# Second cross-attention of a fused network: projection pieces between a step's halves, and two buffers for an unused output

## The chip, the core and the metric

The kernel runs on one core of a Trainium2 chip. A core has TensorE (PE; its weight loads are listed as PEld), VectorE (DVE), ScalarE (ACT), GpSimd (POOL) and SyncE (SP, which here only issues DMAs). Each engine works through its own queue in order; engines wait for each other by semaphores. Products land in PSUM, which has eight banks. The metric is the device time of one execution in microseconds (us). Before the change it is 2459.25 us, the median of 3 runs (2456.62 to 2461.36).

## What is computed

The network has twelve blocks over x (128 tokens of 256). Four of them are cross-attentions over a context of 12,544 keys. The change concerns the second, whose reference, cut to what matters, is:

```python
K = (K_in @ Wk + bk)  # K_in = V_in = context, 12544 x 256; 16 heads of 16
V = (V_in @ Wv + bv)
Q = (Q_in @ Wq + bq)  # Q_in = layernorm(x), 128 x 256
KQ = einsum('bhld,bhpd->bhlp', K, Q) / sqrt(16)
KQ = KQ + mask_pad.reshape(b, 1, l, 1) + mask_attn.T.reshape(1, 1, l, lp)
alpha = softmax(KQ, axis=2)              # over the 12544 keys
O = einsum('bhlp,bhld->bhpd', alpha, V)
return O.transpose(0, 2, 1, 3).reshape(b, lp, 256) @ Wo + bo
```

`mask_attn` is a matrix of 128 x 12544 that is added to the scores of every head. The other three cross-attentions have no such matrix, and so need no addition to each score tile.

## The kernel before

Everything is fp32 and stays on one core. `cross` (from L355) runs one cross-attention. It takes four heads at a time, called a unit, and the keys in tiles of 512: 4 units of 25 tiles, or 100 tiles. The softmax needs each row's maximum before it can exponentiate, so each tile is scored twice:

- `score_s` (L470) computes scores with queries on the partitions, only to find the maximum over the tile for each head. In the second attention (`side`) VectorE adds the mask tile `f` and takes the maximum in one custom instruction (L491); its elementwise result goes to a tile named `junk`, which nobody reads. The profile shows L491 as CUSTOM_DVE_ANT_0 followed by DVE_READ_ACCUMULATOR2_ANT, which writes the maximum.
- `score_t` (L518) computes the same scores with keys on the partitions, 27 tiles later (`lead = NST + 2`, L364), when the unit's maxima are known and have been put into the queries by `lower` (L510). VectorE adds the transposed mask tile `g` (L541), and ScalarE exponentiates (L546).
- `values` (L572) multiplies the exponentials of the tile before with the value tiles (L588), and VectorE adds the result to a sum (L592, L594).

Each tile is one step of the loop at L618. In a step that does both kinds of scoring, `scores` (L549) works in two halves. The first scores heads 2 and 3 for the maxima and heads 0 and 1 for the exponentials; the second does the reverse. A half issues all its products and then all its drains: two L491 and two L541 on VectorE, two L546 on ScalarE. Steps 0 to 26 do maxima alone, steps 27 to 99 both, steps 100 to 126 exponentials alone. A head has 16 rows plus some for mask and maximum in a strip of 32, so four heads fill PE's 128 rows, and products of different heads can run side by side.

The keys and values themselves must be projected from the context. That work is cut into pieces, listed for all four attentions in `self.jobs`, and `pump` (L142) issues as many pieces as it is told. A key piece (`keys`, L201) projects 128 features for 512 keys: four matmuls with all 128 rows of PE (L315), an eviction on ScalarE (L209), and after every second piece a store to DRAM from GpSimd (L212). A value piece (`values`, L214) projects 256 keys: eight matmuls, an eviction (ScalarE in the second attention, L232), and a store after two pieces (L237). The second attention first pumps what is left of its own pieces and then pieces of the third, at a rate written out in L1316.

The order is written by hand: inside `tc.manual_schedule()` (L615) the instructions stand on each engine in the order in which the code issues them. In a step before the change this is: fetches for two tiles ahead, both halves of `scores`, `lower` at the end of a unit, the pieces, `values`.

PSUM banks are dealt out in rotation: `bank` (L135) gives the next of eight. A matmul that writes a bank waits until the engine that drains what lay there is done. A step with one piece takes ten banks: four for the first half, four for the second, one for the piece, one for `values`.

```python
sets = [[(score_s, km, (2, 3)), (score_t, ke, (0, 1))],
        [(score_s, km, (0, 1)), (score_t, ke, (2, 3))]]
for part in sets:
    parts = [make(k, heads) for make, k, heads in part]
    for products, _ in parts:
        products()
    for _, drain in parts:
        drain()
```

Of the kernel before, what the change touches and what calls it, by code (L numbers as in the profile page):

```python
# [25 lines left out]
NST = -(-S2 // ST)  # L26
# [51 lines left out]
class Net:  # L78
# [276 lines left out]
    def cross(self, name, side=False, project=True, rate=()):  # L355
# [11 lines left out]
        with ExitStack() as es:  # L367
# [8 lines left out]
            def rows(u):  # L376

                at = 32 * (width * u % 4)
                return slice(at, at + 32 * width)
# [40 lines left out]
            def fetch_k(k):  # L420

                u, i = divmod(k, NST)
                if u >= units:
                    return
                s, m = i * ST, min(ST, S2 - i * ST)
                if s % SB == 0:
                    b = s // SB
                    self.until(name, b, "k")
                    n = min(SB, S2 - b * SB)
                    clear(NSB * u + b + 2)  # L430
                    t = kts[(NSB * u + b) % held]
                    nc.sync.dma_start(
                        out=t[1::32, :n],
                        in_=self.mask_rows[name][:, s : s + n].to_broadcast([4, n]))
                    for j in range(width):
                        at, h = 32 * j + 2, width * u + j
                        nc.sync.dma_start(out=t[at : at + 16, :n],
                                          in_=self.kx[name, b][16 * h : 16 * h + 16, :])
                    kt[u, b] = t
                if side:  # L440
                    f = ep.tile([P, ST], F32, name=f"{name}_f{k}", tag="f", bufs=3)
                    nc.sync.dma_start(out=f[:, :m], in_=self.io["fside"][:, s : s + m])
                    ft[k] = f
# [21 lines left out]
            def tile_of(u, j):  # L465

                at = 32 * ((width * u + j) % 4)
                return slice(at, at + 32)

            def score_s(k, heads):  # L470

                u, i = divmod(k, NST)
                s, m = i * ST, min(ST, S2 - i * ST)
                if u not in mxs:
                    mxs[u] = pool.tile([P, width, NST], F32, name=f"{name}_mxs{u}", tag="mxs",
                                       bufs=2)
                t, at = kt[u, s // SB], s % SB
                banks = {j: self.bank(f"{name}_s{k}_{j}") for j in heads}

                def products():  # L480
                    for j in heads:
                        r = tile_of(u, j)
                        nc.tensor.matmul(banks[j][:, :m], qb[u][r, :], t[r, at : at + m],  # L483
                                         start=True, stop=True)

                def drain():
                    for j in heads:
                        if side:
                            junk = ep.tile([P, ST], F32, name=f"{name}_j{k}_{j}", tag="junk",
                                           bufs=1)  # L490
                            nc.vector.tensor_tensor_reduce(  # L491
                                out=junk[:, :m], in0=banks[j][:, :m], in1=ft[k][:, :m], scale=1.0,
                                scalar=-3.0e38, op0=ALU.add, op1=ALU.max,
                                accum_out=mxs[u][:, j, i : i + 1])
                        else:
                            nc.vector.tensor_reduce(out=mxs[u][:, j, i : i + 1],  # L496
                                                    in_=banks[j][:, :m], axis=AX.X, op=ALU.max)
                return products, drain

            def raised(k):  # L500

                u, i = divmod(k, NST)
                if i == NST - 1:
                    mx = self.small.tile([P, width], F32, name=f"{name}_mx{u}", tag="mx")
                    nc.vector.tensor_reduce(out=mx, in_=mxs[u], axis=AX.X, op=ALU.max)
                    nc.vector.tensor_scalar(
                        out=lows[u % 2][:, rows(u)].rearrange("p (j r) -> p j r", r=32)[:, :, 0],
                        in0=mx, scalar1=-1.0, scalar2=None, op0=ALU.mult)

            def lower(u):  # L510

                r = rows(u)
                ps = self.bank(f"{name}_mr{u}")
                nc.tensor.matmul(ps[:, :P], lows[u % 2], self.ident, start=True, stop=True)
                nc.vector.tensor_tensor(out=qb[u][r, :], in0=qb[u][r, :], in1=ps[r, :P],
                                        op=ALU.add)
# [29 lines left out]
                        nc.scalar.activation(e[:, j, :m], src, AF.Exp)  # L546
                return products, drain

            def scores(ke, km):  # L549

                if ke is None and km is None:
                    return
                heads = tuple(range(width))
                if ke is None:
                    sets = [[(score_s, km, heads)]]
                elif km is None:
                    sets = [[(score_t, ke, heads)]]
                elif width == 2:
                    sets = [[(score_s, km, heads), (score_t, ke, heads)]]
                else:  # L560
                    sets = [[(score_s, km, (2, 3)), (score_t, ke, (0, 1))],
                            [(score_s, km, (0, 1)), (score_t, ke, (2, 3))]]
                for part in sets:
                    parts = [make(k, heads) for make, k, heads in part]
                    for products, _ in parts:
                        products()
                    for _, drain in parts:
                        drain()
                if km is not None:
                    raised(km)  # L570
# [41 lines left out]
            due, total, waiting = 0.0, units * NST, []  # L612
            n_k = 2 * NST
            n_own = n_k + S2 // 256
            with tc.manual_schedule():  # L615
                for k in (0, 1):
                    fetch_k(k)
                for at in range(total + lead + 3):  # L618
                    fetch_k(at + 2)
                    fetch_v(at + 2 - lead)  # L620
                    ke = at - lead if 0 <= at - lead < total else None
                    km = at if at < total else None
                    scores(ke, km)
                    if 0 < at <= total and at % NST == 0:
                        lower(at // NST - 1)


                    left = sum(1 for (n, _, _), _ in self.jobs if n == name)
                    goal = min(n_k, 2 * (at + 6))
                    if at >= lead - 6:  # L630
                        goal = min(n_own, n_k + 2 * (at - lead + 7))
                    self.pump(min(left, max(0, goal - (n_own - left))))
                    phase = max(0, at - 2) // NST
                    due += rate[phase] if phase < len(rate) else 0.0
                    while due >= 1.0:
                        self.pump(1)
                        due -= 1.0


                    while waiting:  # L640
                        u, i = divmod(waiting[0], NST)
                        n = NST - i if NST - i < 2 * batch else batch
                        last = waiting[0] + n - 1
                        if ke is not None and ke - last < behind - batch + 1:
                            break
                        if last > waiting[-1]:
                            break
                        values(waiting[:n])
                        waiting = waiting[n:]
                    if ke is not None:  # L650
                        waiting.append(ke)
                    u, i = divmod(at - lead - 2 - NST, NST)
                    if i == 0 and 0 <= u < units:
                        finish(u)
# [728 lines left out]
def _device_arrays(I):  # L1383
# [15 lines left out]
    def cross(name, q, k, v, o=None):  # L1399
        a[f"w_{name}"] = cat(*(_padded(q.T).T,) if o is None else (_padded(q.T).T, o))  # L1400
        a[f"w_{name}_kv"] = cat(k, v)

    cross("l0x", I["L0_xattn_q_w"].T, I["L0_xattn_k_w"].T, I["L0_xattn_v_w"].T)
    cross("l1x", *(I[f"L1_xattn_W{k}"] for k in "qkvo"))
    cross("l2x", *(I[f"L2_xattn_w{k}"] for k in "qkvo"))
    cross("l3x", *(I[f"L3_xattn_W{k}"] for k in "qkvo"))
    a["w_l0a"] = cat(I["L0_attn_Wq"].T, I["L0_attn_Wk"].T, I["L0_attn_Wv"].T)
# [73 lines left out]
```

## Time and profile before

| what | us |
|---|---|
| median of 3 runs | 2459.25 |
| the profiled execution | 2463.49 |
| its span, first to last instruction | 2461.6 |
| PE busy (modelled ends) | 2324.9 |
| VectorE busy | 1628.7 |
| ScalarE busy | 1150.0 |
| second attention, from its first L491 to its last L541 | 649.5 to 1298.4 |
| of it, steps that do both kinds of scoring | about 752 to 1208 |

The page of a profile gives, for one execution, the busy time of each engine and then groups of instructions: line, engine, operation, what is written and read, the count, the busy time and the mean length of one, and after the bar the time in which the engine sat idle just before them and what ended it. The waits list who waited for whom, in total. The timeline lists instructions in order of time, with start and length. Windows give the busy time of each engine in chosen stretches, with the share of full speed that TensorE's clock was granted and the busy share of the DMA engines. The busy time of PE is no measure of how full it is, since its ends are modelled and overlap; distances between starts are more telling.

### The profile page before, as it was taken

To read this page: it belongs to the slowest core of one execution; us is meant where nothing else is said; L and a number is where in the kernel's file an instruction comes from. 1 tells how busy PE (TensorE), PEld (TensorE's weight loads), DVE (VectorE), ACT (ScalarE), POOL (GpSimd) and SP (SyncE) were. 2 spreads that over 40 slices of the span, in tenths; PEclk is the share of its full clock that TensorE was granted. 3 is DMA by queue.
4 is the path that set the end of the run, shared out by engine and by line. 5 is a ranking of instruction groups with operands and counts; after the bars stand their busy time and mean duration, and the time that the engine had idled before them with its cause. 6 is when DMAs were issued, how large, how long until landed. Compare 5 with 4: busy or idle time off the path is not lost. (4 is left out here: it accounts for less than half of the span.)

```text
span 2461.6 us, 75645 instructions
## 1 busy us (share of the span) xinstructions
PE 2324.9 (94%) x32103; PEld 1716.3 (70%) x32103; DVE 1628.7 (66%) x3503; ACT 1150.0 (47%) x2109; POOL 246.2 (10%) x465
## 2 busy tenths in 40 slices
PE   6999999999899999999998998899999679999969
PEld 3358888876447876666777744478888546888848
DVE  2566688522477788888886734788882769888331
ACT  2213366773214445545582254046668302666832
POOL 2221100001221100000101111200000121000001
PEclk9999999999999999999999998999999888999979
DMA  7766633237779867777765675553322633333216
GB/s 273 263 222 215 208 97 93 69 118 278 259 232 303 275 216 223 229 227 219 223 198 191 211 254 195 165 151 92 92 78 68 231 109 101 91 91 97 63 44 225
DMA packets 191119, 430.29 MB, mean 175 GB/s; under 512 B 26908, under 2 KB 83248, under 8 KB 186688
## 3 DMA queue, kind: packets, MB, share of 16 engines
q1 hardware_dynamic: 154576, 269.26, 36.9%
q0 software_dynamic: 35840, 154.94, 16.8%
q8 instruction: 256, 4.19, 0.7%
q10 hardware_dynamic: 368, 1.25, 0.1%
q14 instruction: 79, 0.65, 0.1%
HBM read 319.18 MB, written 106.16 MB: 173 GB/s over the span
## 5 line engine op out<-in xcount | busy, mean ns | idle before, releaser
L546 ACT ACTIVATE l1x_e<-l1x_e 128x512 f32<-128x512 f32 (+1 forms) x400 | 240.5, 622 | 248.2 <-DVE l1x_e L541 248.2
L491 DVE CUSTOM_DVE_ANT_0 l1x_j<-l1x_s,l1x_f 128x512 f32<-128x512 f32 (+1 forms) x400 | 271.1, 678 | 80.9 <-PE l1x_t L533 29.9
L496 DVE TENSOR_REDUCE l0x_mxs<-l0x_s 128x1 f32<-128x512 f32 (+1 forms) x400 | 244.3, 672 | 97.5 <-PE l0x_s L483 66.0
L546 ACT ACTIVATE l0x_e<-l0x_t 128x512 f32<-128x512 f32 (+1 forms) x400 | 203.2, 594 | 176.9 <-PE l0x_t L533 173.4
L546 ACT ACTIVATE l3x_e<-l3x_t 128x512 f32<-128x512 f32 (+1 forms) x400 | 203.4, 594 | 167.2 <-PE l3x_s L483 92.6
L496 DVE TENSOR_REDUCE l2x_mxs<-l2x_s 128x1 f32<-128x512 f32 (+1 forms) x400 | 243.8, 672 | 36.7 <-PE l2x_t L533 24.3
L546 ACT ACTIVATE l2x_e<-l2x_t 128x512 f32<-128x512 f32 (+1 forms) x400 | 203.4, 594 | 137.2 <-PE l2x_t L533 133.5
L496 DVE TENSOR_REDUCE l3x_mxs<-l3x_s 128x1 f32<-128x512 f32 (+1 forms) x400 | 243.4, 671 | 33.1 <-PE l3x_t L533 23.9
L541 DVE TENSOR_TENSOR l1x_e<-l1x_t,l1x_g 128x512 f32<-128x512 f32 (+1 forms) x400 | 249.9, 671 | 11.3 <-PE l1x_t L533 8.3
L483 PE MATMUL l3x_s<-l3x_kt,l3x_qb 32*128 32x512 f32 (+1 forms) x800 | 202.8, 652 | 7.1 <-DMA l3x_kt<-l3x_kx 3.5
L533 PE MATMUL l1x_t<-l1x_qb,l1x_kt 32*128 32x128 f32 x3136 | 204.3, 284 | 2.7 <-ACT l1x_vs L232 0.6
L483 PE MATMUL l1x_s<-l1x_kt,l1x_qb 32*128 32x512 f32 (+1 forms) x800 | 203.2, 618 | 3.4 <-DMA l1x_kt<-l1x_kx 3.2
L533 PEld LDWEIGHTS l1x_t<-l1x_qb,l1x_kt 32*128 32x128 f32 x3136 | 171.6, 187 | 36.5 <-ACT l2x_ks L209 19.6
L483 PE MATMUL l2x_s<-l2x_kt,l2x_qb 32*128 32x512 f32 (+1 forms) x800 | 189.5, 620 | 5.8 <-DMA l2x_kt<-l2x_kx 5.3
L483 PE MATMUL l0x_s<-l0x_kt,l0x_qb 32*128 32x512 f32 (+1 forms) x800 | 183.5, 614 | 5.6 <-ACT l0x_ks L209 3.8
L533 PE MATMUL l3x_t<-l3x_qb,l3x_kt 32*128 32x128 f32 x3136 | 181.1, 281 | 0.0
L533 PE MATMUL l2x_t<-l2x_qb,l2x_kt 32*128 32x128 f32 x3136 | 180.0, 280 | 0.0
L533 PE MATMUL l0x_t<-l0x_qb,l0x_kt 32*128 32x128 f32 x3136 | 178.9, 279 | 0.0
L533 PEld LDWEIGHTS l3x_t<-l3x_qb,l3x_kt 32*128 32x128 f32 x3136 | 160.8, 187 | 6.5 <-issue 5.0
L533 PEld LDWEIGHTS l2x_t<-l2x_qb,l2x_kt 32*128 32x128 f32 x3136 | 159.8, 186 | 5.9 <-issue 5.0
L533 PEld LDWEIGHTS l0x_t<-l0x_qb,l0x_kt 32*128 32x128 f32 x3136 | 159.1, 186 | 5.9 <-issue 5.0
L588 PEld LDWEIGHTS l1x_p<-l1x_e,l1x_vt 128*32 128x32 f32 x3136 | 82.0, 110 | 51.3 <-DVE l1x_mxs L491 18.9
(599 smaller groups left out, 3665.8 us busy)
## 6 DMA issues: line engine op xcount, KB each, us to landing
l1x_f<-in_fside SPq DMA_DIRECT2D x96, 256.0 KB
l1x_g<-in_fsideT SPq DMA_DIRECT2D x96, 256.0 KB
w<-in_w_l3f POOLq DMA_DIRECT2D x16, 1024.0 KB, 5.1
l0x_vx<-l0x_vs POOLq DMA_DIRECT2D x24, 544.0 KB, 5.5
l0x_vt<-l0x_vx SPq DMA_DIRECT2D x48, 272.0 KB
l1x_vx<-l1x_vs POOLq DMA_DIRECT2D x24, 544.0 KB, 5.9
l1x_vt<-l1x_vx SPq DMA_DIRECT2D x48, 272.0 KB
l2x_vx<-l2x_vs POOLq DMA_DIRECT2D x24, 544.0 KB, 4.8
```

Of the source, the lines that this page charges most:

```text
L483: nc.tensor.matmul(banks[j][:, :m], qb[u][r, :], t[r, at : at + m], start=True, stop=True)
L491: nc.vector.tensor_tensor_reduce(out=junk[:, :m], in0=banks[j][:, :m], in1=ft[k][:, :m], scale=1.0, scalar=-3.0e38, op0=ALU.add, op1=ALU.m ...
L496: nc.vector.tensor_reduce(out=mxs[u][:, j, i : i + 1], in_=banks[j][:, :m], axis=AX.X, op=ALU.max)
L533: nc.tensor.matmul(banks[j][:, a * P : (a + 1) * P], t[r, at + a * P : at + (a + 1) * P], qb[u][r, :], start=True, stop=True)
L541: nc.vector.tensor_tensor(out=e[:, j, :m], in0=src, in1=gt[k][:, : m // P, :].rearrange("p a q -> p (a q)"), op=ALU.add)
L546: nc.scalar.activation(e[:, j, :m], src, AF.Exp)
L588: nc.tensor.matmul(ps[32 * c : 32 * c + 32, :P], lhs, rhs, start=n < 4, stop=n >= len(todo) - 4, skip_group_check=True)
```

## The change

It has two parts, both for the second attention alone.

The tile `junk` gets two buffers in place of one. It is 512 fp32 values for each of 128 partitions, and the memory is there.

The pieces of a step are counted before `scores` is called. In steps that do both kinds of scoring, half of them (rounded up) are issued between the first half and the second, and the others where they were, before `values`. So a single piece moves wholly between the halves, and of two pieces one does. The number of pieces in each step stays. Outside the second attention, and in its steps with one kind of scoring, `inner` is 0.

```diff
                         if side:
                             junk = ep.tile([P, ST], F32, name=f"{name}_j{k}_{j}", tag="junk",
-                                           bufs=1)
+                                           bufs=2)
...
-            def scores(ke, km):
+            def scores(ke, km, between):
...
-                for part in sets:
+                for n, part in enumerate(sets):
+                    if n == 1:
+                        between()
                     parts = [make(k, heads) for make, k, heads in part]
...
-                    scores(ke, km)
-                    if 0 < at <= total and at % NST == 0:
-                        lower(at // NST - 1)
...
-                    self.pump(min(left, max(0, goal - (n_own - left))))
                     phase = max(0, at - 2) // NST
                     due += rate[phase] if phase < len(rate) else 0.0
-                    while due >= 1.0:
-                        self.pump(1)
-                        due -= 1.0
+                    pieces = min(left, max(0, goal - (n_own - left))) + int(due)
+                    due -= int(due)
+                    inner = (pieces + 1) // 2 if side and ke is not None and km is not None else 0
+                    scores(ke, km, lambda: self.pump(inner))
+                    if 0 < at <= total and at % NST == 0:
+                        lower(at // NST - 1)
+                    self.pump(pieces - inner)
```

## The prediction

> **What bounds the kernel now.** The change touches only the second attention, so I read the page's engine rows and groups first, then busy time in windows of that stage, then its timeline, then its waits.
>
> ```profile
> PE 2324.9 (94%) x32103; PEld 1716.3 (70%) x32103; DVE 1628.7 (66%) x3503; ACT 1150.0 (47%) x2109; POOL 246.2 (10%) x465
> ...
> L491 DVE CUSTOM_DVE_ANT_0 l1x_j<-l1x_s,l1x_f 128x512 f32<-128x512 f32 (+1 forms) x400 | 271.1, 678 | 80.9 <-PE l1x_t L533 29.9
> ```
>
> PE at 94% is a share of modelled ends, so it can't settle what binds. L491 has 80.9 us of idle VectorE before it in 400 instructions, of which PE explains 29.9. The windows:
>
> ```profile
> core 0: us, PE busy (x) PEld busy (x) DVE busy (x) ACT busy (x) POOL busy (x), PEclk, DMA share, GB/s
> 650.00:674.00 24.00, 23.54 (x78) 8.61 (x76) 19.92 (x59) 4.54 (x7) 4.49 (x6) 1.00 0.68 221
> 800.00:871.40 71.40, 71.40 (x918) 60.09 (x911) 54.48 (x132) 35.64 (x64) 9.71 (x20) 1.00 0.83 264
> 884.30:921.20 36.90, 36.41 (x480) 26.88 (x479) 34.78 (x95) 16.60 (x30) 0.75 (x1) 0.95 0.66 201
> 966.10:1028.00 61.90, 61.43 (x771) 39.16 (x769) 53.02 (x132) 31.48 (x53) 3.20 (x6) 1.00 0.75 233
> ```
>
> These are four regimes of one stage: maxima alone; two value pieces a step; no piece; on average 1.2 key pieces a step. In the third VectorE is busy 94%, in the fourth 86%. The timeline shows a step of the fourth (start, length, what; in brackets the engine's idle time and what ended it):
>
> ```profile
> 1034.32 0.69 DVE L491 CUSTOM_DVE_ANT_0 l1x_j<-l1x_s,l1x_f 128x512 f32<-128x512 f32 x1 [0.73 <-PE l1x_t L533]
> ...
> 1034.94 0.08 DVE L491 DVE_READ_ACCUMULATOR2_ANT l1x_mxs<- 128x1 f32 x1
> 1035.17 0.69 DVE L491 CUSTOM_DVE_ANT_0 l1x_j<-l1x_s,l1x_f 128x512 f32<-128x512 f32 x1
> ...
> 1035.78 0.08 DVE L491 DVE_READ_ACCUMULATOR2_ANT l1x_mxs<- 128x1 f32 x1
> 1035.78 1.28 DVE L541 TENSOR_TENSOR l1x_e<-l1x_t,l1x_g 128x512 f32<-128x512 f32 x2
> ...
> 1040.29 0.67 ACT L209 ACTIVATE l2x_ks<-l2x_k,cols 128x512 f32<-128x512 f32 x1
> ...
> 1041.01 0.97 PEld L533 LDWEIGHTS l1x_t<-l1x_qb,l1x_kt 32*128 32x128 f32 x16 [0.95 <-ACT l2x_ks L209]
> ```
>
> Two losses stand here. VectorE: after the read of the accumulator the next L491 starts 0.23 us later (1034.94 to 1035.17), but an L541 at once (1035.78). PE: the second half's t products wait until 1041.01 for ScalarE to empty the bank of the previous step's key piece; ScalarE does that only at 1040.29, behind all four exponentials. The waits confirm it as a habit (in total, times, longest):
>
> ```profile
> PEld l1x_t L533 <- ACT l2x_ks L209: 19.6, 30, 0.9
> ```
>
> **Durations** (distances between starts in the timeline). VectorE: an L491 0.616, plus 0.226 more if another L491 follows; an L541 0.60; the sum L594 0.195. A step: 4 x 0.616 + 2 x 0.226 + 4 x 0.60 + 0.195 = 5.51. That is exactly the distance of steps without a piece (895.27 to 900.77). PE: a half alone 1.07 (the maxima regime, 670.49 to 671.56), both halves back to back 1.96 (849.66 to 851.62); a key piece 1.91 (1035.74 to 1037.65); a value piece 1.83 (3.65 for two, 851.62 to 855.27); L588 1.01. ScalarE: an exponential 0.61, a key eviction 0.67.
>
> With these I laid out the order of before by hand: each operation starts when its engine is free, its PSUM bank emptied (eight in rotation) and its input ready. Five key steps with 1, 1, 1, 1, 2 pieces come to 31.0 us; the trace has 5.51, 6.35, 5.51, 6.35, 7.21 = 30.93. Value steps come to 6.66 and 7.28; the trace has 6.63 and 7.35. So the bank account describes this stage, and I use it for the change.
>
> **Second buffer.** No instruction is added. With one buffer, the second L491 of a pair overwrites what the first wrote, and in the program of before it waits for the accumulator read in front of it; with two its wait looks at least one read further back. No L491 without that wait stands in the trace, so the cost is bounded: at most 0.226 saved (it then starts as an L541 does); at least nothing (if the custom instruction must wait for the read anyway); in between 0.15 (the 0.08 of the read stays). I take 0.226, from the nearest row, 1035.78. VectorE's step: 5.51 - 2 x 0.226 = 5.06. The Trainium skill speaks against it: VectorE: DVE Perf Modes, section The DRAIN you can't avoid, says that a semaphore between chained instructions costs nothing extra, since the next one waits for the pipe in any case. By it this part is worth 0; by 1034.94 against 1035.78 it is worth 0.45 a step. The measured row decides; the rule stays as a rival.
>
> **Pieces between the halves.** Number and order of pieces stay: a lone piece goes wholly between the halves, of two pieces one does. VectorE's and GpSimd's orders are unchanged, so its buffer clears and stores of keys and values pass nothing. On SP one load of weights (l3x_kvw, 0.5 MB) moves ahead of five small loads of keys, needed about two steps later: 0. On PE the piece stands before the second half, whose products VectorE waits for; on ScalarE its eviction stands between the first two exponentials and the last two, so behind it wait those two and the next step's L588. The eviction's own input, the piece, ends before the first exponentials do, so it adds only its 0.67.
>
> Laid out for one key piece, from the first half's start: halves 0 and 2.98, piece 1.07, L588 4.05, next step 5.06. VectorE drains the first half from 1.14 to 3.58, waits to 4.12 for the second half, drains it to 6.56, then L594 to 6.76; the next first half was ready at 6.20. VectorE so needs 5.06 too. The piece's eviction now comes 2.4 us earlier than behind four exponentials. Banks: next step's first half takes the piece's bank for a t tile, which costs 0.49 every other step when VectorE runs late. Five steps give 5.62, 5.08, 5.55, 5.08, 6.93 = 28.26, instead of 30.93.
>
> Against this, TensorEngine Tiling (Array Packing), section Key Properties, says that changing the tiling mode drains TensorE; a piece between the halves adds one change from 32 rows to 128 and back. The row's price is 2 x 1.07 - 1.96 = 0.18 a step; by the rule alone no number follows. Taking the halves at half of 1.96 instead gives 27.86.
>
> **Sum over the stage** (step starts read off VectorE's timeline):
> - 46 key steps, 921.3 to 1207.7: 46/5 x (30.93 - 28.26) = 24.6.
> - 17 value steps from 757: mean 6.99, after 2 x 1.07 + 3.66 + 1.01 = 6.81, plus 0.02 of waits: 17 x 0.16 = 2.7.
> - 8 steps without a piece: 8 x 0.45 = 3.6.
> - Maxima alone, 27 steps: the first 8 take 3.36 = 4 x 0.84, PE needs 1.07 + 1.91 = 2.98: 8 x 0.38 = 3.0. After that PE waits for keys (at 674.94 for a load issued at 670.40) and for a context load (714.66); neither hangs on VectorE, so 0 (at most 8 more).
> - The last 27 steps hold no L491 and keep their order: 0.
>
> Sum 33.9. The profiled execution took 2463.5 (span 2461.6 and 1.9 around it): 2429.6. The median of the runs is 4.2 lower: 2425.4, so **2426**. What is late next: PE in the value steps, both engines about equally in the key steps.
>
> **Rivals.**
> 1. The custom instruction is held by the read anyway. Key steps 29.16, so 9.2 x 1.77 = 16.3, and value steps 2.7: 19.0, **2440**. For: the rule above; no unheld L491 in the trace. Against: 1035.78. Chance 0.12.
> 2. Only the buffer pays: the moved piece makes a new wait as long as the old. With the old order and two buffers the layout gives 29.67: 11.6 + 3.6 + 3.0 + 17 x 0.25 = 22.4, **2437**. Chance 0.11.
> 3. More than laid out: halves at 0.98, 27.86 (28.2), value steps 6.63 (6.1), maxima 6, none 3.6: 44, **2415**. Against: the DMA share, 0.83 in the value steps. Chance 0.12.
> 4. Slower: the second half starves VectorE. If the next first half may not run ahead, because the piece's eviction comes too late for its t tile, a step becomes 1.14 + 1.91 + 1.07 + 2.44 + 0.20 = 6.76 against a mean of 6.19: 46 x 0.57 = 26 lost, 7 gained elsewhere, **2478**. It decides where the wait for the eviction grows from a mean of 0.25 to over 0.78 a step. For: ScalarE keeps order, and exponentials wait for VectorE. Against: ScalarE is busy half the time. Chance 0.06.
> 5. No change, because other waits take it all: **2459**, chance 0.03.
>
> **Chances.** The likeliest case has 0.56, its own range 2419 to 2433 (the 0.15 and 0.226 of the buffer, halves between 0.98 and 1.07). Cases 1 to 3 widen it: 2413 to 2443. 0.2% is 4.9 us, about what a measurement can tell from no change. Faster 0.91, same 0.03, slower 0.06.
>
> **What would show it.** Right: the start after an accumulator read is 0 to 0.08 us later for L491 too; steps without a piece 5.06; five key steps about 28.3; the wait of L533's weights for L209 gone or on the first half; L491 waiting about 0.5 us for PE in the middle of a step; value steps all alike near 6.8. Wrong: 0.23 stays (case 1); key steps still alternate with over 6.2 (case 2); L491's wait in mid-step over 1 us (case 4). TensorE's clock was halved for 3.41 us at 1077 (one step took 9.7); if denser work brings more of that, each costs some 2 us.

## The result, and the profile after

The changed kernel took 2430.81 us, the median of 4 runs (2424.94 to 2440.84), against 2458.07 for the kernel before, measured beside it (4 runs, 2456.62 to 2461.36). The ratio is 0.9891, with a 95% interval from 0.9856 to 0.9927. The forecast was 2426, with a range from 2413 to 2443.

The profiled execution took 2424.94, its span 2422.8. That span is 38.8 shorter than the one before, but only 30.9 of it lies in the second attention (649.4 to 618.5, from its first L491 to its last L541). The other 7.9 lie where no instruction was touched, and a second profile of the same kernel, e0_again below, does not have them: there the stretch after the stage takes 1162.5, as before it took 1162.8. So at most the 30.9 are the change's; in e0_again the stage takes 624.6, which is 24.8 less than before.

From the page of the changed kernel (line numbers behind L561 are two higher than before, so L588 is now L590 and L594 is L596):

```profile
PE 2289.4 (94%) x32103; PEld 1699.7 (70%) x32103; DVE 1611.5 (67%) x3503; ACT 1150.0 (47%) x2109; POOL 246.8 (10%) x465
...
L491 DVE CUSTOM_DVE_ANT_0 l1x_j<-l1x_s,l1x_f 128x512 f32<-128x512 f32 (+1 forms) x400 | 253.0, 676 | 74.8 <-PE l1x_t L533 39.7
```

Counts are the same. L491's mean length is too (676 ns against 678), but its group is busy 18.1 us less: the two of a pair now overlap in the record. VectorE waits longer for L533, 39.7 against 29.9: it got faster, and PE is late more often. The windows of the changed kernel, for value steps, steps without a piece, and key steps:

```profile
767.50:866.00 98.50, 98.50 (x1230) 78.84 (x1230) 74.35 (x182) 47.80 (x84) 13.59 (x28) 1.00 0.85 274
879.20:908.40 29.20, 28.84 (x418) 22.43 (x416) 28.61 (x82) 13.90 (x25) 0.00 (x0) 0.94 0.69 213
942.20:1026.80 84.60, 84.60 (x1153) 55.57 (x1152) 77.46 (x197) 47.22 (x79) 4.81 (x9) 1.00 0.83 254
```

VectorE's share rose from 94% to 98% in the steps without a piece, and from 86% to 92% in the key steps. In the value steps it is 75%, after 76%: there it does not bind. The timeline of the changed kernel shows a value step (start, length, what; in brackets idle time and releaser; PE's L533 beside L483 is left out):

```profile
838.13 1.99 PE L315 MATMUL l1x_v<-l1x_kvw,l1x_cv 128*128 128x256 f32 x8
838.19 0.69 DVE L491 CUSTOM_DVE_ANT_0 l1x_j<-l1x_s,l1x_f 128x512 f32<-128x512 f32 x1 [0.73 <-PE l1x_t L533]
...
838.80 0.08 DVE L491 DVE_READ_ACCUMULATOR2_ANT l1x_mxs<- 128x1 f32 x1
838.80 0.69 DVE L491 CUSTOM_DVE_ANT_0 l1x_j<-l1x_s,l1x_f 128x512 f32<-128x512 f32 x1
...
840.06 0.70 PE L483 MATMUL l1x_s<-l1x_kt,l1x_qb 32*128 32x512 f32 x2
...
841.16 1.99 PE L315 MATMUL l1x_v<-l1x_kvw,l1x_cv 128*128 128x256 f32 x8
...
843.08 1.08 PE L590 MATMUL l1x_p<-l1x_e,l1x_vt 128*32 128x128 f32 x32
...
844.09 0.70 PE L483 MATMUL l1x_s<-l1x_kt,l1x_qb 32*128 32x512 f32 x2
```

Two things are to be seen. The second L491 starts with the accumulator read, at 838.80, no longer 0.23 after it. And PE never pauses, yet its starts are further apart than forecast: piece to half 1.93 (838.13 to 840.06), half to piece 1.10, piece to L590 1.92. The same view of PE in a key step:

```profile
979.05 0.70 PE L483 MATMUL l1x_s<-l1x_kt,l1x_qb 32*128 32x512 f32 x2
...
980.15 1.08 PE L590 MATMUL l1x_p<-l1x_e,l1x_vt 128*32 128x128 f32 x32
981.16 0.70 PE L483 MATMUL l1x_s<-l1x_kt,l1x_qb 32*128 32x512 f32 x2
...
982.26 1.98 PE L315 MATMUL l2x_k<-l2x_ck,l2x_kvw 128*128 128x512 f32 x4
984.18 0.70 PE L483 MATMUL l1x_s<-l1x_kt,l1x_qb 32*128 32x512 f32 x2
```

That is 1.10 + 1.01 + 1.10 + 1.92 = 5.13 without a gap: PE sets these steps, with VectorE's 5.03 just behind. The wait of L533's weights for the key eviction fell from 19.6 us in 30 times to 0.6 in two:

```profile
PEld l1x_t L533 <- ACT l2x_ks L209: 0.6, 2, 0.4
```

Stretch by stretch, from the starts on VectorE (us):

| steps | before | after | one step or five, before | after |
|---|---|---|---|---|
| 0 to 26, maxima alone | 102.3 | 99.4 | | |
| 27 to 44, mostly value pieces | 127.0 | 125.0 | 7.35 and 6.63 in turn | 7.07 |
| 45 to 51, no piece | 37.0 | 34.9 | 5.50 | 5.03 |
| 52 to 98, key pieces | 292.0 | 269.0 | five: 30.93 | 28.21 |
| 99 to 126, exponentials alone (99 still both) | 91.1 | 90.3 | | |

The value steps got slower, 7.07 against a mean of 6.99. Their stretch is shorter only because of its first two steps, which took 15.2 before, with TensorE's clock halved at 760, and 12.0 after. Without a halved clock there, e1 and e3 below take 13.0 for them in the old order.

In the maxima steps VectorE now waits for the mask tile `f`. Its waits there (in total, times, longest), before and after:

```profile
DVE l1x_j L491 <- DMA l1x_f<-in_fside: 0.5, 1, 0.5
```

```profile
DVE l1x_j L491 <- DMA l1x_f<-in_fside: 14.3, 7, 3.0
```

One key step, step 93, grew from 7.01 to 10.40. It holds the first value piece of the third attention, and PE stands waiting for that piece's context load:

```profile
1140.63 0.64 PE L533 MATMUL l1x_t<-l1x_qb,l1x_kt 32*128 32x128 f32 x8
1144.07 3.45 PE L315 MATMUL l2x_v<-l2x_kvw,l2x_cv 128*128 128x256 f32 x8 [2.81 <-DMA l2x_cv<-in_ctxT]
```

The load is issued early in the step ahead, as before. Before, PE came to the piece 8.2 us after the issue and found the data there; now it is ready for it after 6.5 us, and the data come after 9.3. The piece then meets a halved clock (3.45 us in place of 1.99). The same wait, of 1.8 to 4.4 us, stands in 11 of the 12 profiles of kernels that move the pieces (e9_four_f has none; in e5_interleaved the profile puts it down to VectorE). It is not in the profile of before, nor in that of e1_buffer_only, which leaves the pieces where they were. So the wait goes with the move, and the forecast has no term for it. Why the data come no sooner, no run shows.

### The profile page after: what moved, and what is told of

It reads as the page before. It is cut to its first block, busy times and chain, and to the rows that moved or that the text cites. A ratio compares the mean times of both kernels' runs of the same rounds, so it can differ in the third digit from the quotient of the medians.

```text
span 2422.8 us, 75640 instructions
## 1 busy us (share of the span) xinstructions
PE 2289.4 (94%) x32103; PEld 1699.7 (70%) x32103; DVE 1611.5 (67%) x3503; ACT 1150.0 (47%) x2109; POOL 246.8 (10%) x465
## 5 line engine op out<-in xcount | busy, mean ns | idle before, releaser
L546 ACT ACTIVATE l1x_e<-l1x_e 128x512 f32<-128x512 f32 (+1 forms) x400 | 240.6, 622 | 219.5 <-DVE l1x_e L541 219.5
L496 DVE TENSOR_REDUCE l0x_mxs<-l0x_s 128x1 f32<-128x512 f32 (+1 forms) x400 | 244.3, 672 | 97.4 <-PE l0x_s L483 66.0
L491 DVE CUSTOM_DVE_ANT_0 l1x_j<-l1x_s,l1x_f 128x512 f32<-128x512 f32 (+1 forms) x400 | 253.0, 676 | 74.8 <-PE l1x_t L533 39.7
L546 ACT ACTIVATE l0x_e<-l0x_t 128x512 f32<-128x512 f32 (+1 forms) x400 | 203.2, 594 | 176.9 <-PE l0x_t L533 173.4
L546 ACT ACTIVATE l3x_e<-l3x_t 128x512 f32<-128x512 f32 (+1 forms) x400 | 203.5, 594 | 166.8 <-PE l3x_s L483 92.3
L546 ACT ACTIVATE l2x_e<-l2x_t 128x512 f32<-128x512 f32 (+1 forms) x400 | 203.3, 594 | 137.3 <-PE l2x_t L533 133.7
L496 DVE TENSOR_REDUCE l2x_mxs<-l2x_s 128x1 f32<-128x512 f32 (+1 forms) x400 | 243.8, 672 | 35.8 <-PE l2x_t L533 23.9
L496 DVE TENSOR_REDUCE l3x_mxs<-l3x_s 128x1 f32<-128x512 f32 (+1 forms) x400 | 243.2, 672 | 33.7 <-PE l3x_t L533 23.9
L541 DVE TENSOR_TENSOR l1x_e<-l1x_t,l1x_g 128x512 f32<-128x512 f32 (+1 forms) x400 | 250.1, 672 | 10.0 <-PE l1x_t L533 9.0
L483 PE MATMUL l3x_s<-l3x_kt,l3x_qb 32*128 32x512 f32 (+1 forms) x800 | 201.4, 653 | 8.3 <-DMA l3x_kt<-l3x_kx 7.8
L483 PE MATMUL l1x_s<-l1x_kt,l1x_qb 32*128 32x512 f32 (+1 forms) x800 | 203.1, 635 | 3.1 <-DMA l1x_kt<-l1x_kx 3.1
L533 PE MATMUL l1x_t<-l1x_qb,l1x_kt 32*128 32x128 f32 x3136 | 202.8, 284 | 0.2
L483 PE MATMUL l2x_s<-l2x_kt,l2x_qb 32*128 32x512 f32 (+1 forms) x800 | 189.6, 617 | 5.5 <-DMA l2x_kt<-l2x_kx 5.0
L483 PE MATMUL l0x_s<-l0x_kt,l0x_qb 32*128 32x512 f32 (+1 forms) x800 | 182.2, 612 | 5.7 <-ACT l0x_ks L209 4.0
L533 PE MATMUL l3x_t<-l3x_qb,l3x_kt 32*128 32x128 f32 x3136 | 181.1, 281 | 0.0
L533 PE MATMUL l2x_t<-l2x_qb,l2x_kt 32*128 32x128 f32 x3136 | 179.9, 280 | 0.0
L533 PE MATMUL l0x_t<-l0x_qb,l0x_kt 32*128 32x128 f32 x3136 | 179.0, 279 | 0.0
L533 PEld LDWEIGHTS l1x_t<-l1x_qb,l1x_kt 32*128 32x128 f32 x3136 | 168.9, 186 | 10.0 <-DVE l1x_e L541 3.2
L533 PEld LDWEIGHTS l3x_t<-l3x_qb,l3x_kt 32*128 32x128 f32 x3136 | 160.8, 187 | 6.5 <-issue 5.0
L533 PEld LDWEIGHTS l2x_t<-l2x_qb,l2x_kt 32*128 32x128 f32 x3136 | 159.8, 186 | 5.9 <-issue 5.0
L533 PEld LDWEIGHTS l0x_t<-l0x_qb,l0x_kt 32*128 32x128 f32 x3136 | 159.2, 186 | 5.9 <-issue 5.0
L590 PE MATMUL l1x_p<-l1x_e,l1x_vt 128*32 128x128 f32 x3136 | 112.5, 278 | 2.0 <-ACT l1x_e L546 1.9
```

Source lines behind the costliest of these rows:

```text
L491: nc.vector.tensor_tensor_reduce(out=junk[:, :m], in0=banks[j][:, :m], in1=ft[k][:, :m], scale=1.0, scalar=-3.0e38, op0=ALU.add, op1=ALU.m ...
L496: nc.vector.tensor_reduce(out=mxs[u][:, j, i : i + 1], in_=banks[j][:, :m], axis=AX.X, op=ALU.max)
L533: nc.tensor.matmul(banks[j][:, a * P : (a + 1) * P], t[r, at + a * P : at + (a + 1) * P], qb[u][r, :], start=True, stop=True)
L541: nc.vector.tensor_tensor(out=e[:, j, :m], in0=src, in1=gt[k][:, : m // P, :].rearrange("p a q -> p (a q)"), op=ALU.add)
L590: nc.tensor.matmul(ps[32 * c : 32 * c + 32, :P], lhs, rhs, start=n < 4, stop=n >= len(todo) - 4, skip_group_check=True)
```

## The experiments

Each kernel computes the whole reference. Diffs are cut, and against the changed kernel unless it is said otherwise. "Five key steps" and "value step" are read from the distances between starts in a stretch that no halved clock touches. Kernels e0 to e3 shared one chip, e4 to e8 another, e8_again to e10 a third, and e11 a fourth.

**e0_again.** No edit: the changed kernel once more, as the measure of what a profile repeats.

> The changed kernel once more, beside the others on one chip. From the trace: key steps 28.2 us for five, value steps 7.07 each, steps without a piece 5.03, the stage 618.5 us from first L491 to last L541 (649.4 before). Theory (two separate losses, each part removes one): 2427 to 2431 us, about 28 to 31 under before. Rival (part of the measured gain is chance in the clock outside the stage): under 25 gained.

2438.92 (2429.82 to 2452.58), before there 2463.75, ratio 0.9904 (0.9875 to 0.9933). Five key steps 28.21, value steps 7.07, no piece 5.03: to 0.01 the same. But the maxima steps took 102.6 (99.4 in the first profile), step 93 took 12.04 (10.40), and the stage 624.6. So steps repeat, and stage lengths differ by some 6 us from one execution to the next. The 28 to 31 expected were missed: 24.8 were gained, 0.2 on the rival's side of its line. The interval, 16.5 to 31, reaches to both sides. Parts below are judged by steps.

**e1_buffer_only.** The order of before, with the second buffer. This diff alone is against the kernel before.

```diff
-                                           bufs=1)
+                                           bufs=2)
```

> Before, with two buffers for the unused output and the old place of the pieces. Theory: VectorE's step falls to 5.03 and the wait of the second half for the eviction stays, so five key steps 29.7 (5.06, 6.3, 5.06, 6.3, 7.0), value steps 6.66 and 6.83, maxima steps as in the changed kernel: about 22 us under before, 2436. Rival (the buffer alone is the change): as fast as the changed kernel, 28 to 31 under before. Rival (the order alone is): no gain.

2441.02 (2439.33 to 2441.86), ratio 0.9905 (0.989 to 0.992). Five key steps 29.54 and 29.73 in turn, 29.63 on average, where the layout gave 29.67; value steps 6.89 and 6.63 in turn; no piece 5.03. The buffer is worth all of its 0.226 per pair. The old loss on PE stays; the waits of this kernel, and its timeline on PE:

```profile
PEld l1x_t L533 <- ACT l2x_ks L209: 14.5, 16, 0.9
```

```profile
991.14 1.04 PE L483 MATMUL l1x_s<-l1x_kt,l1x_qb 32*128 32x512 f32 x4
992.29 1.16 PE L533 MATMUL l1x_t<-l1x_qb,l1x_kt 32*128 32x128 f32 x16
993.38 1.98 PE L315 MATMUL l2x_k<-l2x_ck,l2x_kvw 128*128 128x512 f32 x4
```

The t products of both halves run together, 1.15 after the s products that they could have lain beside. Its time is not told from e0_again's. The steps say why: against the whole change it loses 46/5 x 1.42 = 13 in key steps and gains 17 x 0.31 = 5 in value steps, 8 us net. Some of that returns in step 93: 6.73 here, where PE does not wait for the context load, against 10.40 and 12.04. What is left is within the intervals.

**e2_order_only.** The moved pieces, with one buffer.

```diff
-                                           bufs=2)
+                                           bufs=1)
```

> The changed kernel with one buffer again. Theory: the second half no longer waits for the eviction, but VectorE's 0.226 us after each accumulator read stays, so steps without a piece 5.51, five key steps 29.2, value steps 7.07 (TensorE without a gap, so the buffer counts for nothing there), maxima steps 3.36: about 15 us under before, 2444. Rival (the order alone is the change): 28 under before.

2450.54 (2443.93 to 2462.76), ratio 0.9942 (0.9922 to 0.9962). Five key steps 29.14 (the layout gave 29.16), no piece 5.49, value steps 7.07. So 5.49 to 5.03 is the buffer's, and 7.07 the order's.

**e3_values_after.** Value pieces stay behind both halves; only key pieces move.

```diff
-                    inner = (pieces + 1) // 2 if side and ke is not None and km is not None else 0
+                    inner = (pieces + 1) // 2 if side and ke is not None and km is not None and not left else 0
```

> The changed kernel, but while pieces of the second attention's own values are left, all pieces stay behind both halves. Theory (two value pieces parted by a half cost TensorE 0.44 us a step more than side by side, and that is more than the eviction wait they save): value steps 6.66 and 6.83 in place of 7.07, key steps unchanged at 28.2 for five, so 5 us faster than the changed kernel. Rival (7.07 comes from transfers or from the bank of the piece, not from the place): value steps stay near 7.07, or key steps after them suffer; no gain.

2431.82 (2428.38 to 2437.87), ratio 0.987 (0.9852 to 0.9889). Value steps 6.89 and 6.63, key steps unchanged at 28.21. Moving value pieces costs 0.31 a step.

**e4_both_between.** Both value pieces of a step stand side by side between the halves.

```diff
-                    inner = (pieces + 1) // 2 if side and ke is not None and km is not None else 0
+                    inner = (pieces if left else (pieces + 1) // 2) if side and ke is not None and km is not None else 0
```

> The changed kernel, but both value pieces of a step stand between the halves, side by side. It tells what makes a value step 7.07. Theory (each change between products of 32 and of 128 rows costs TensorE about 0.1 us, so what counts is how often the kinds alternate): two pieces side by side 3.66, two halves of 1.10, L588 1.01: 6.87 to 6.95 a step, key steps unchanged at 28.2, so 2 to 3 us under the changed kernel in the stage. Rival (the bank of the piece or its eviction makes it): 7.07 stays or grows.

2433.33 (2421.49 to 2441.21), ratio 0.9883 (0.9839 to 0.9928). Every value step takes 6.87. Its timeline on PE:

```profile
829.94 0.70 PE L483 MATMUL l1x_s<-l1x_kt,l1x_qb 32*128 32x512 f32 x2
...
831.04 3.72 PE L315 MATMUL l1x_v<-l1x_kvw,l1x_cv 128*128 128x256 f32 x16
834.69 0.70 PE L483 MATMUL l1x_s<-l1x_kt,l1x_qb 32*128 32x512 f32 x2
...
835.79 1.08 PE L590 MATMUL l1x_p<-l1x_e,l1x_vt 128*32 128x128 f32 x32
836.80 0.70 PE L483 MATMUL l1x_s<-l1x_kt,l1x_qb 32*128 32x512 f32 x2
```

Two pieces side by side take 3.65, parted 3.85; the halves still take 1.10 each. PE's packed value step takes 6.63 where halves, pieces and L590 each stand in one run (three changes of kind a step, counting the one into the next step), 6.87 with four changes, 7.07 with five. Each further change costs 0.24 and 0.20.

**e5_interleaved.** One buffer, but each half's drains alternate, so that an L541 stands between two L491.

```diff
-                def drain():
-                    for j in heads:
+                def drain(n=None):
+                    for j in heads if n is None else heads[n : n + 1]:
...
-                                           bufs=2)
+                                           bufs=1)
...
+                    if side and len(parts) == 2:
+                        for j in range(2):
+                            for _, drain in parts:
+                                drain(j)
+                        continue
```

> The changed kernel with one buffer again, but a half's drains alternate: L491, L541, L491, L541. Theory (what costs is only the wait of an L491 for the accumulator read directly in front of it, not the buffer as such): an L541 stands in between, the wait is over when the second L491 comes, steps without a piece 5.03 and five key steps about 28.2, as with two buffers. In the maxima steps there is no L541, so they stay at 3.36. Rival (the custom instruction is slower when it writes the same tile again): 5.49 and 29.1 as with the order alone.

2434.63 (2432.5 to 2440.75), ratio 0.9895 (0.987 to 0.9921). Five key steps 28.21, no piece 5.03: what two buffers give, from one. VectorE's timeline:

```profile
986.82 0.08 DVE L491 DVE_READ_ACCUMULATOR2_ANT l1x_mxs<- 128x1 f32 x1
986.82 0.69 DVE L541 TENSOR_TENSOR l1x_e<-l1x_t,l1x_g 128x512 f32<-128x512 f32 x1
987.42 0.68 DVE L491 CUSTOM_DVE_ANT_0 l1x_j<-l1x_s,l1x_f 128x512 f32<-128x512 f32 x1
```

The loss was the wait on the instruction directly ahead, not the shared memory: with one instruction between, the wait is met before it is reached. In the maxima steps, where nothing can stand between, each step still takes 3.36.

**e7_all_four.** The pieces go between the halves in all four attentions.

```diff
-                    inner = (pieces + 1) // 2 if side and ke is not None and km is not None else 0
+                    inner = (pieces + 1) // 2 if ke is not None and km is not None else 0
```

> The changed kernel with the pieces between the halves in all four cross-attentions. The other three show no wait of the second half for an eviction (their evictions need no addition first). Theory: there the new place only costs what alternating costs, 0.2 to 0.4 us in each step with pieces, about 70 steps each: 30 to 60 us slower than the changed kernel, and slower than before. Rival (the place is good in itself): as fast or faster than the changed kernel.

2447.47 (2438.74 to 2457.29, 11 runs), ratio 0.9942 (0.9925 to 0.9959). The price was right and the count wrong: it was expected to be slower than before, and is faster. In the first attention the value steps go from 6.63 to 7.07 as forecast, but there are only 17 of them, so they cost 17 x 0.44 = 7.5 us and not 30 or more. The stage grows by 10.3 (487.9 to 498.2, from its first L496 to its last L546); 1.8 of that stand in its first step, which no moved piece touches. The third attention grows by 2.5, the fourth by 0.1. In the first attention, where PE sets the value steps, the move only costs.

**e8_evict_first.** PE's order and the banks are those of before (only at the end of a unit do the pieces now stand ahead of `lower`). The pieces are issued behind both halves' products but ahead of the second half's drains, so that only ScalarE's order changes: it empties the piece's bank before the last two exponentials.

```diff
-                    if n == 1:
-                        between()
                     parts = [make(k, heads) for make, k, heads in part]
                     for products, _ in parts:
                         products()
+                    if n == 1:
+                        between()
...
-                    inner = (pieces + 1) // 2 if side and ke is not None and km is not None else 0
+                    inner = pieces if side and ke is not None and km is not None else 0
```

> The changed kernel, but the pieces stand behind the products of the second half and ahead of its drains: TensorE's and the banks' order is that of before, and only ScalarE evicts the piece ahead of the second half's exponentials. Theory (the loss was ScalarE's order, and TensorE's order was only a way to change it): the eviction wait goes as it does with the changed kernel, without the cost of parting the halves. Laid out: five key steps 27.3, value steps 6.63, without a piece 5.03: about 15 us less in the stage than the changed kernel, near 2415. Rival (the second half has to come later on TensorE for the bank to be free): the wait for the eviction returns, key steps alternate at over 6.1 as with the buffer alone.

2422.44 (2418.9 to 2424.32), ratio 0.984 (0.9818 to 0.9863). Five key steps 27.44, value steps 6.63 without exception, no piece 5.03. The steps came as laid out. The time did not, 2422 against 2415; the stage is 606.2, which is 12 and 18 us less than in the two profiles of the changed kernel. Its timeline on ScalarE:

```profile
981.38 1.23 ACT L546 ACTIVATE l1x_e<-l1x_e 128x512 f32<-128x512 f32 x2 [1.39 <-DVE l1x_e L541]
982.68 0.69 ACT L209 ACTIVATE l2x_ks<-l2x_k,cols 128x512 f32<-128x512 f32 x1
983.80 1.23 ACT L546 ACTIVATE l1x_e<-l1x_e 128x512 f32<-128x512 f32 x2 [0.43 <-DVE l1x_e L541]
```

L209 starts 0.04 after its piece's last product could have ended (980.66 + 1.98 on PE), and the two exponentials behind it wait for VectorE anyway. The wait of L533's weights for L209 is gone here as well, with no piece between halves on PE. So the useful part of the move was where the eviction stands on ScalarE. Step 93 waits 2.5 for its load here too, and takes 10.56.

**e8_again, e9_four_f, e10_f_first.** These go on from e8, into the maxima steps, which a faster VectorE hardly shortened. e8_again has no edit. e9_four_f gives the mask tile `f` a fourth buffer (room for it comes from a narrower type for the unused output). e10_f_first loads `f` ahead of the keys on SP.

```diff
-                    f = ep.tile([P, ST], F32, name=f"{name}_f{k}", tag="f", bufs=3)
+                    f = ep.tile([P, ST], F32, name=f"{name}_f{k}", tag="f", bufs=4)
...
-                            junk = ep.tile([P, ST], F32, name=f"{name}_j{k}_{j}", tag="junk",
+                            junk = ep.tile([P, ST], mybir.dt.bfloat16, name=f"{name}_j{k}_{j}", tag="junk",
```

> The version with the pieces behind the second half's products and ahead of its drains, once more, beside two that build on it. As before: 2419 to 2424 us, 606 us in the stage, maxima steps 0 to 26 together 99 to 100 us.

> The same with four buffers in place of three for the mask tile f; to make room the unused output is bf16. With two buffers for the unused output, L491 waits 11 to 14 us in all for f, 7 times, nearly all in the maxima steps (0.5 before). Theory (f is late because its load waits for a buffer that VectorE frees only one step earlier, and holds up the key loads behind it on SP): most of it goes, maxima steps 90 to 94 us, 5 to 9 us faster than the version it builds on. Rival (f is late because it stands behind the key loads, which wait for GpSimd and the piece's store): f and keys come as late as now, under 2 us gained.

> The same with three buffers, but the load of f stands ahead of the key loads of its step on SP. Theory (buffer): the wait for VectorE now stands ahead of the key loads, so the keys come later; maxima steps as long as now or longer. Rival (place on SP): f no longer waits for the key loads, L491's waits for f go, maxima steps shorter by up to 10 us unless TensorE then waits for keys.

On one chip (before there 2459.09): e8_again 2423.19 (2417.53 to 2432.16), ratio 0.9861 (0.9838 to 0.9883); e9_four_f 2418.72 (2411.74 to 2436.51), 0.9853 (0.9821 to 0.9886); e10_f_first 2429.09 (2427.47 to 2436.97), 0.9888 (0.9865 to 0.9912). The first 18 steps took 61.5, 60.7 and 59.5, the 27 steps 100.9, 98.7 and 104.6. The fourth buffer takes SP's wait on L491 from 8.6 to 2.2, and no measurable time off the kernel. Of the 104.6, some 6 are the clock's: one step of 10.64, where e8_again has 4.72, met a halved clock of 6.8 us, and two value pieces took 5.91 there in place of 3.65:

```profile
730.04 5.91 PE L315 MATMUL l1x_v<-l1x_kvw,l1x_cv 128*128 128x256 f32 x16
```

The earlier load takes L491's wait for `f` from 8.7 to 2.7, but its wait for PE's scores rises from 24.2 to 33.6, and 5.6 of that lie in the step of the halved clock. SP's wait for GpSimd falls from 28.4 to 16.0, and its wait for VectorE at the load of `f` rises from 8.6 to 19.1: SP stands elsewhere instead. At most 2 us came of it in the first 18 steps, so neither the buffer of `f` nor its place was the main cause; both loads stand behind something else. SP's waits in the maxima steps name it; first of the changed kernel, then of e11_clear_late:

```profile
SPq L410 <- POOL l1x_kt L409: 27.6, 14, 4.2
```

```profile
SPq L410 <- POOL l1x_kt L409: 6.1, 6, 1.4
```

**e11_clear_late.** From e8. SP stood waiting for GpSimd to clear a key tile that is needed only two blocks later. That clear, and the load of ones behind it, are issued after the loads.

```diff
-                    clear(NSB * u + b + 2)
+                    clear(NSB * u + b + (0 if side else 2))
...
                     ft[k] = f
+                if side and s % SB == 0:
+                    clear(NSB * u + s // SB + 2)
```

> The kernel of e8 (pieces ahead of the second half's drains, both halves' products first), with GpSimd's clearing of a later key tile moved behind the key loads and the load of f, so that SP no longer stands for it. Theory (in the maxima steps SP's wait of some 28 us in all for GpSimd's clear of the key tile holds up the key loads and the loads of f): the first 27 steps fall from about 100 us to 94 to 97 (TensorE alone would take about 3 us for each of the first 18, 54 us against the 60 to 61 measured), VectorE's waits for f fall under 5 us, and the time is 3 to 6 us below e8's 2422 to 2423. Rival (the loads or TensorE are late of themselves, and what is gained is given back at the next context load): the 27 steps stay within 2 us of 100, and the time within 2 us of e8's.

2415.26 (2412.15 to 2421.65), before there 2462.78, ratio 0.9812 (0.9785 to 0.9839). The 27 steps took 93.1, against 99.6 and 100.9 in the two profiles of e8. The first 18 of them, which end before the clock is first halved in the stage, took 54.4, against 60.6 and 61.5; that is about what PE alone needs (18 x 2.98 = 53.6). Five key steps and value steps are e8's. VectorE's wait for `f` fell to 4.6. This is the kernel with the lowest median and ratio here, and its interval lies below both of the changed kernel's. Against e8 the intervals overlap (0.9818 to 0.9863); it is the stretch's length that speaks for a further gain.

## Why the prediction was right, and where it was not

- **Second buffer, 0.226 a pair: right, at its upper bound.** The next L491 starts 0 ns after the read, the pitch from read to read is 0.61, and steps without a piece take 5.03 (forecast 5.06). The sentence on semaphores that the forecast took from the Trainium skill (VectorE: DVE Perf Modes, section The DRAIN you can't avoid) would have made this 0. The same section adds that a next instruction that is not held starts earlier, and that is what these rows show. A wait on the instruction directly ahead was not free here: e1 and e2 show 0.46 a step for the buffer alone, and e5 the same from another order. Rival 1 is out.
- **Key steps: right.** Forecast 5.62, 5.08, 5.55, 5.08, 6.93 = 28.26; measured 5.64, 5.13, 5.45, 5.13, 6.86 = 28.21. The bank account holds for each part alone too (e1, e2) and for e8, laid out at 27.3 and measured at 27.44. Over the stretch 23.0 came of 24.6: step 93 grew by 3.4, by the wait for its load and the halved clock behind it, and before a step of 9.7 stood at the clock halved at 1077, which takes 6.37 now. The late load is a term that the forecast left out: for these steps it weighed one load of weights on SP and no context load. Rival 2 (29.67) is out by the steps, though e1's time alone could not have told it.
- **Why the pieces must go between the halves: right on the wait, not on what has to move.** The forecast treated the place on PE and the place on ScalarE as one move. e8 parts them: ScalarE's place gives all of it, and PE's place only costs (27.44 against 28.21, and 6.63 against 7.07).
- **Value steps, 17 x 0.16 = 2.7: wrong sign.** The term was 2 x 1.07 + 3.66 + 1.01 = 6.81. It took the two pieces at their pair's price, though the change parts them. Measured: 2 x 1.10 + 1.93 + 1.92 + 1.01 = 7.06. Of the 0.26 missed, 0.20 lies in the parted pieces and 0.06 in the halves, whose 1.07 was read in the maxima steps, from a run of eight L483 that is no half of such a step. Instead of 2.7 gained, 17 x 0.08 = 1.4 were lost in regular steps. The rule weighed in the forecast, from the Trainium skill (TensorEngine Tiling (Array Packing), section Key Properties: a change of tiling mode drains TensorE), bore here more than the 0.18 taken for it: 0.20 to 0.24 for each of two added changes. What TensorE does in that time no run shows.
- **No piece, 3.6: mechanism right.** 0.47 a step was saved, against 0.45; the seven steps 45 to 51 shortened by 2.1, with a halved clock in both executions.
- **Maxima steps, 3.0: about 2 came, and not as forecast.** The first profile has 102.3 to 99.4, but the second has 102.6. Over all the profiles here, the three with one buffer (before, e2, e5) have 102.1 to 102.4; the eight with two that leave the loads alone have 98.3 to 102.6, on average 100.2. The steps whose inputs are there did get shorter, but loads came late in their place: VectorE's wait for `f` in that stretch is 14.3 in 7 waits, where it was 0.5 in one. What holds the stretch is for the most part SP's wait for GpSimd: e11 removes most of it, and 6 to 8 us go. That loads bind, which don't hang on VectorE's speed, was right; it holds from the first steps on, not from the ninth.
- **Last 27 steps, 0:** 0.8 shorter, which is no more than executions differ.
- **Sum:** 33.9 forecast, 30.8 in the stage (2.9 + 2.0 + 2.1 + 23.0 + 0.8). By medians the gain was 27.3 with the first chip and 24.8 with the second, so the forecast was some 6 to 9 us too high. About 4 of that is the value steps' term (2.7 + 1.4), about 1 the maxima, and some 3 to 5 the late load in step 93 (10.40 and 12.04 against 7.01); this is an estimate, since a halved clock before, at 1077, makes up for part of it. That the stage of the first profile came within 3 us of the forecast's sum is in part luck: two steps of before met a halved clock, at 760 and 1077, and those of the changed kernel did not.
- **Rival 3 (more than laid out):** it wanted halves at 0.98 and value steps of 6.63. The changed order cannot give it; e8's order does, with 27.44 and 6.63.
- **Rival 4 (the second half starves VectorE):** VectorE does wait in mid-step, 0.52 at 841.21 in a value step and 0.28 and 0.51 in two key steps, about the 0.5 forecast and under the 1 us named. The move turns to loss where VectorE has nothing to gain, as in the value steps and in e7's first attention.

## What to carry to other kernels

When a product waits for a bank that another engine has not emptied, look first at where the emptying stands in that engine's queue; moving it there (e8) cost nothing, while moving the producer on TensorE brought more alternation between kinds of matmul, at 0.2 us a change. A reduction whose elementwise output nobody reads still makes the next one wait if both write one tile back to back: a second buffer, or another instruction between them, removes that. Price a piece that is to be moved as it will stand, alone, not from a row where it stood beside its like. And when work moves ahead, ask of each load whether it still lands in time: one that was there when PE came for it before was late by 2.8 us afterwards.

## What the runs showed of the hardware that was not expected

- A change from one kind of matmul to another costs time even when PE never waits: the same work of a value step takes 6.63, 6.87 or 7.07 with three, four or five changes (e8, e4, the changed kernel). With each added change a run of like products is also cut in two; no run parts the one from the other.
- The wait of an L491 on the accumulator read directly ahead cost 0.226 us; with one L541 between them, or another output tile, it cost 0.
- TensorE's clock was halved for 3.4 or 6.8 us at a time in the stage (elsewhere for up to 34), in most kernels near the same places (about 713, 895 and 1140), and for 161 to 192 us in all of an execution. A step that meets one takes up to 12.4 us, other waits included. How many fall into the stage changes from one execution to the next (one in e9_four_f, three in the changed kernel), and much of the spread between runs of one kernel may come from that; it was not tested.
- The halving near 1140 goes with PE's wait for the context load in step 93. Of the 11 profiles with that wait, nine have a halved clock beside it and a step of 10.0 to 12.4; e5 (a wait of 1.8) and e11 (3.3) have none there, with steps of 7.8 and 9.7. The three without the wait (before, e1, e9) have none there either, with steps of 6.2 to 7.0. That the wait brings the halving on is likely and not shown: no run changes the wait alone, and e11 speaks against a fixed rule.
